# Sparse graph attention on one core: deep and own blocks take turns, first own blocks are weighed by VectorE, and several small steps come later

## The chip, the cores and the metric

The kernel runs on one core of one Trainium2 chip. A time is the device time of one execution in microseconds (us). TensorE (PE in the profile) multiplies matrices, VectorE (DVE) and ScalarE (ACT) work element by element, GpSimd (POOL) here mostly issues indirect DMAs (gathers and scatters of rows by a list of indices), and SyncE (SP) issues plain DMAs. Each engine takes its instructions in the order in which they were written, and waits in front of one whose inputs or buffers are not ready.

## The reference

`x` is 16 x 1024 x 512, `adj` is 1024 x 1024 of zeros and ones, and the same `adj` holds for all 16 batches. There are 8 heads of 64.

```
q = (x @ Wq + bq), k = (x @ Wk + bk), v = (x @ Wv + bv)      # per batch, 8 heads of 64
scores = q . k / 8 + (1 - adj) * -1e9
attn = softmax(scores)
out = attn @ v
x = layernorm(x + out @ Wo + bo)                              # no weight, eps 1e-5
```

`adj` is thin: most queries have few keys, some have dozens. So the kernel never forms the 1024 x 1024 scores.

## The kernel before, in words

**Blocks.** Queries are ranked by their number of keys and cut into 8 tiles of 128. Tile t has `OWN[t]` *own blocks*, (2, 1, 2, 3, 4, 5, 5, 7): own block i holds the i-th key of each of the 128 queries, so keys and values are gathered by one indirect DMA (`kvg`, L1230) and the query tile is read once. What queries of tiles 6 and 7 have beyond that is packed into `BLOCKS` = 1 and 5 *deep blocks* of 128 (query, key) pairs. A deep block also gathers its queries (`qg`, L1184), and its 128 rows are added into the right queries by two TensorE products with a 0/1 matrix (`add_up`, the `sum` at L1301 and L1302). Tile 1 has one key per query and needs no scores. That makes 34 blocks for batches 0, 1 and every odd batch, 32 for the other even ones (their tile 0 is handled with the next batch's), 530 in all.

**A block's way.** `products` multiplies q and k (DVE, `qk`, L1251), `scores` sums by head (DVE, L1255), `exponentials` takes exp (ACT, L1266), `weigh` multiplies the gathered values by it: either 8 ScalarE instructions, one for each head (L1276), or one VectorE instruction (L1280); `by_act` (L1268) decides. For an own block `add_own` then adds it to the tile's sum (DVE, L1292); for a deep block `add_up` does it on TensorE. After a tile's last block `normalise` divides, and `turn` transposes the result (PE, `poT`, L1336) for the product with Wo (`po`, L790), which `finish` and `complete` turn into the output: residual, `ysq` sum of squares, `variance`, `power` (a POOL instruction, L1113), `shift`, `norm_out` and a scatter (L1125).

**Fronts.** For later batches the kernel meanwhile computes q, k and v: `load_x` gathers a tile of x (POOL, L1001), `transpose_x` transposes it (`pxT`, L748), and `pair(b, j)` makes k and v of two tiles at once by a Strassen-like scheme of 7 half products into the accumulators `x`, `z` and `pp` (L947), with ScalarE and VectorE taking sums in between (`out_e`, `out_w`, `out_g`, `out_k1`, `out_v1`, `out_v0`; L960 to L979), and q by a plain product (`pq`, L790). In the pair with j = 0 the tile 1 has no q product from batch 1 on, and even batches from 2 on have no q product for tile 0 either. k and v go to DRAM, from where the blocks gather them. `mean_pe` (L858) is one product that takes the mean of a batch's v (used for queries without keys); its row goes to DRAM by SP, and only then is the batch marked in `set_up`, without which none of its blocks may be gathered.

**Order.** All order is written out by a loop over turns (L1470): `n` runs from -39 to the end, and turn n works on block n. In a turn come: exp of block n+3, products of n+4, gathers up to n+8 (up to n+11 when the fronts are done), VectorE's weighing of n+1, the own sum of n, scores of n+4, `normalise` if a tile began, then what `later(k, ...)` put k turns ahead, ScalarE's weighing of n+2, what `later_last` put there, and `add_up` of n. Last, TensorE's other work is dealt out: each turn adds its `paced` share to a `credit`, and units of fronts or of `po` are written while the credit is positive; things in `urgent` (transposes, the mean) come in between. A unit whose inputs' turn has not come (`ready`) ends the dealing for that turn. Generators (`edges`, `bias_setup`, `ranks`, `lookups`), which build the key lists in the turns before block 0, advance by one `yield` a turn.

The last pair of a batch thus sets `mean_pe` two turns after its second `send`, `load_x` is called in the turn after the transposes that free its buffer, and at the end of each batch come the 5 deep blocks of tile 7 in a row.

Of the kernel before, what the change touches and what calls it, by code (L numbers as in the profile page):

```python
# [177 lines left out]
def kernel(  # L178
# [75 lines left out]
    with ExitStack() as main:  # L254
# [139 lines left out]
        def bias_setup():  # L394
            bk_bc = work.tile([P, D], F32, tag="y", name="bk_bc", bufs=Y_BUFS)
            broadcast(bk_bc, bk)
            yield
            n4 = small.tile([P, NPAIR], F32, name="bk_norms", bufs=1)
            nc.vector.tensor_tensor(bk_bc, bk_bc, bk_bc, op=OP.mult)
            nc.vector.tensor_reduce(n4, bk_bc.rearrange("p (h d) -> p h d", d=P), axis=AX.X, op=OP.add)  # L400
            nc.vector.tensor_reduce(bk_norm, n4, axis=AX.X, op=OP.max)
            n8 = small.tile([P, HEADS], F32, name="bq_norms", bufs=1)
            nc.vector.tensor_tensor(bk_bc, bq_bc, bq_bc, op=OP.mult)
            nc.vector.tensor_reduce(n8, bk_bc.rearrange("p (h d) -> p h d", d=HD), axis=AX.X, op=OP.add)
            nc.vector.tensor_reduce(bq_norm, n8, axis=AX.X, op=OP.max)
            yield
            pb = fill_psum("pb")
            nc.tensor.transpose(pb[:, 0:2 * NPAIR], bias_rows, ident[:2 * NPAIR, :2 * NPAIR])
            nc.tensor.transpose(pb[:, 2 * NPAIR:3 * NPAIR], bv_rows, ident[:NPAIR, :NPAIR])
            yield  # L410
            nc.vector.tensor_copy(bias_qk, pb[:, 0:2 * NPAIR])
            bv_col = one.tile([P, NPAIR], F32, name="bv_col")
            nc.vector.tensor_copy(bv_col, pb[:, 2 * NPAIR:3 * NPAIR])
            bvb = work.tile([P, NPAIR, P], F32, tag="y", name="bvb", bufs=Y_BUFS)
            nc.vector.tensor_copy(bvb, bv_col[:, :, None].to_broadcast([P, NPAIR, P]))
            yield
            pb = fill_psum("pb3")
            for c in range(NPAIR):
                nc.tensor.matmul(pb, bvb[:, c, :], W["o"][:, c, :], start=(c == 0), stop=(c == NPAIR - 1))
            yield  # L420
            nc.vector.tensor_tensor(bo_bc, pb, bo_bc, op=OP.add)
# [209 lines left out]
        def edges(t):  # L631
# [38 lines left out]
                nc.vector.tensor_tensor(check[:, 2 * NT + 1:2 * NT + 2], ranked[:, t, 1:2], st[:, 0:1], op=OP.subtract)  # L670

            nc.vector.tensor_scalar(deg, ranked[:, t, 1:2], -float(K), 0.0, op0=OP.add, op1=OP.max)
            yield
            po = fill_psum(f"poff_{t}")
            nc.tensor.matmul(po[:, 0:1], before, deg, start=True, stop=True)
            yield
# [66 lines left out]
        def transpose_x(b, t):  # L743
            def pe():
                xs = X.pop((b, t))
                p = fill_psum(f"pxT_{b}_{t}")
                for c in range(NPAIR):
                    nc.tensor.transpose(p[:, ts(c, P)], xs[:, ts(c, P)], ident)  # L748

                def out():  # L750
                    XT[b, t] = work.tile([P, D], F32, tag="xT", name=f"xT_{b}_{t}", bufs=4)
                    nc.scalar.copy(XT[b, t], p)
                    n = b * NT + t + 3
                    if t == 0 and b >= PAIRED_FROM:
                        if not merged(b):
                            BOTH[b // 2] = work.tile([P, 2, NPAIR, P], F32, tag="place", name=f"both_{b}", bufs=1)
                        nc.scalar.copy(
                            BOTH[b // 2].rearrange("p w c (h n) -> p h c w n", h=2)[:, b % 2],
                            p.rearrange("p (c w n) -> p c w n", c=NPAIR, w=2),
                        )  # L760
                        sq = work.tile([P, D], F32, tag="ysq", name=f"sq_x_{b}", bufs=1)
                        nc.scalar.activation(sq[0:LONE, :], xs[0:LONE, :], AF.Square, accum_out=x_norm[0:LONE, b:b + 1])
                    if b * NT + t in STORED:
                        nc.sync.dma_start(residual[b * NT + t], xs)
                        later(2, lambda: load_x(n // NT, n % NT))
                    else:
                        load_x(n // NT, n % NT)
                    if t % 2 and (b, t) != (0, 1):
                        later(1, combine)

                def combine():
                    s = [work.tile([P, HD2], F32, tag=f"s{i}", name=f"s{i}_{b}_{t}", bufs=1 + i // 4) for i in (1, 2, 3, 4)]
                    x0, x1 = XT[b, t - 1], XT[b, t]
                    nc.vector.tensor_tensor(s[0], x1[:, 0:HD2], x1[:, HD2:D], op=OP.add)
                    nc.vector.tensor_tensor(s[2], x0[:, 0:HD2], x1[:, 0:HD2], op=OP.subtract)
                    nc.vector.tensor_tensor(s[1], s[0], x0[:, 0:HD2], op=OP.subtract)
                    nc.vector.tensor_tensor(s[3], x0[:, HD2:D], s[1], op=OP.subtract)
                    SX[b, t // 2] = s

                later(1, out)  # L780

            return [(TRANSPOSE, pe, lambda: (b, t) in X)]
# [24 lines left out]
        def pair(b, j):  # L807
# [25 lines left out]
            def send(i):  # L833
                assert b < PAIRED_FROM or gathered[0] >= start[max(0, b // 2 * 2 - 2)]
                kv = KV[b, tt[i]]
                rows, base = kv_of(b)
                for lo, hi in ((0, LONE), (LONE + P, 2 * P)) if b and tt[i] == 0 else ((tt[i] * P - (LONE if b and tt[i] == 1 else 0), None),):
                    hi = lo + P if hi is None else hi
                    part = slice(0 if lo % P == 0 or hi - lo == P else LONE, P if hi - lo == P or lo else LONE)
                    later(1, lambda lo=lo, hi=hi, part=part: nc.sync.dma_start(rows[base + lo:base + hi, :], kv[part, :]))  # L840
                R["sent"] = R.get("sent", 0) + 1
                if R["sent"] == 2:
                    later(1, add_v)
                    if j == NT // 2 - 1:
                        later(2, lambda: urgent.append(mean_pe))

            def add_v():
                kv = [KV.pop((b, t))[:, D:] for t in tt]
# [136 lines left out]
            units = []  # L985
            units += unit("x", lambda: a(0, 0), B11, True, out_e, None)
            units += unit("p6", s(2), T2, True, out_w, None)
            units += q0
            units += unit("x", lambda: a(0, 1), B21, False, lambda: out_k(0, R["x"]), "e")
            units += unit("p7", s(3), T3, True, out_g, None)  # L990
# [94 lines left out]
        def complete(b, t, p, plain):  # L1085
# [46 lines left out]
            if single:  # L1132
                late = 1 if fronts else 0
                later(2 + late, variance)
                later(3 + late, power)
                later(4 + 2 * late, shift)
                later_last(5 + 2 * late, norm_out)
            elif second:
                later(3, variance)
                mate_shift, mate_norm_out = half.pop()[1]  # L1140

                def powers():
                    nc.gpsimd.tensor_tensor(
                        st2[:, :, 3:4], st2[:, :, 2:3], neg_half[:, :, None].to_broadcast([P, 2, 1]), op=OP.pow
                    )

                def shifts():
                    mate_shift()
                    shift()

                later(4, powers)
                later(6, shifts)
                later_last(6, mate_norm_out)
                later_last(7, norm_out)
            else:
                later(3, variance)
                mine = half[0]
                mine.append((shift, norm_out))

                def alone():  # L1160
                    if half and half[0] is mine:
                        half.pop()
                        power()
                        later(2, shift)
                        later_last(3, norm_out)

                later(6, alone)
# [2 lines left out]


        KG, QG, PV, PSUM, QT, RDEN, V1 = {}, {}, {}, {}, {}, {}, {}
        blocks = [(b, t, i) for b in range(B) for t in tiles_of(b) if t != ONE_KEY for i in range(OWN[t] + BLOCKS[t])]
        start = [min(n for n, block in enumerate(blocks) if block[0] == b) for b in range(B)] + [len(blocks)]

        def load_more():
# [90 lines left out]

        def by_act(n):  # L1268
            b, t, i = blocks[n]
            return 0 < i < OWN[t] or n < total - NBT and (n % 2 == 0 or n < NBT // 2)  # L1270

        def weigh(n):
            v, pv = KG.pop(n), PV[n]
# [174 lines left out]
        with tc.manual_schedule():  # L1448
# [21 lines left out]
            while n < total or plan or rest or urgent or done or finishing or spilled or lone_tiles or not guarded:  # L1470
# [50 lines left out]
                    reload(*spilled.pop(0), reloads)  # L1521
                    reloads, last_reload = reloads + 1, n
                first_unit = True
                while credit > 0 or urgent:
                    if urgent and not (first_unit and fronts):
                        urgent.pop(0)()
                        continue
                    if (
# [2 lines left out]
                    ):  # L1531
                        finishing = finish(*done.pop(0))
                        last_finish = n
                    units = finishing or fronts
                    if not units:
                        if urgent:
                            urgent.pop(0)()
# [52 lines left out]
```

## Time and profile before

| | us |
|---|---|
| median of 3 runs (1903.19 to 1907.76) | 1906.49 |
| the profiled execution's own time | 1892.33 |
| its span, first to last instruction | 1890.4 |
| PE busy | 1815.1 (96%) |
| DVE busy | 1700.6 (90%) |
| ACT busy | 1531.7 (81%) |
| POOL busy | 1267.4 (67%) |
| mean granted TensorE clock | 0.989 |

Busy time is the union of an engine's instructions. A matrix product in 32-bit floats appears as two records of some 596 ns each that overlap; in the chain of waits eight records take 3.43 us, so one 128x512x128 product occupies TensorE for about 0.86 us. "Idle before, and what ended it" is the time in which an engine had nothing running, put down to the instruction whose end let it go on.

### The profile page before, as it was taken

The page shows a single profiled execution, that of the slowest core. Times are in us where ns is not written, and L with a number is a line of the kernel's source. Part 1 is how long each engine was busy: PE and PEld are TensorE (multiplying, and loading weights), DVE is VectorE, ACT ScalarE, POOL GpSimd, SP SyncE. Part 2 cuts the span into 40 slices and gives each one's busy share as a digit, 9 for nine tenths or more (in the row PEclk, how much of TensorE's full clock was granted, in tenths as well). Part 3 has the DMA queues.
Part 4 walks back from the last instruction along what each step waited for, and adds up shares of the span by engine and source line. Part 5 has one row for each costly group of instructions (what it writes and reads, how often), then busy time and mean ns, then how long its engine had stood idle before and what let it go on. Part 6 is the DMA issues. An engine that isn't in the chain of part 4 may idle for free. (4 is left out here: it accounts for less than half of the span.)

```text
span 1890.4 us, 25101 instructions
## 1 busy us (share of the span) xinstructions
PE 1815.1 (96%) x5149; PEld 878.2 (46%) x5149; DVE 1700.6 (90%) x3484; ACT 1531.7 (81%) x6016; POOL 1267.4 (67%) x1189
## 2 busy tenths in 40 slices
PE   7989999999999999999999999999999999999995
PEld 3434444444545454444445444444445444444442
DVE  6888889999999999899899989899999999997874
ACT  3627869979888988979798978989898989886794
POOL 1367766777677676757677676767666777656774
PEclk9989999999999999999999999999999999999997
DMA  7357787988889898888889898999889899989993
GB/s 280 114 168 226 233 307 227 315 295 294 308 287 316 305 328 283 305 288 307 312 292 335 271 334 274 314 304 310 301 307 326 293 356 310 314 277 340 334 319 117
DMA packets 188149, 544.63 MB, mean 288 GB/s; under 512 B 32602, under 2 KB 32622, under 8 KB 187986
## 3 DMA queue, kind: packets, MB, share of 16 engines
q0 software_dynamic: 116400, 382.82, 60.6%
q1 hardware_dynamic: 68510, 154.30, 21.8%
q10 hardware_dynamic: 3076, 5.82, 0.9%
q14 instruction: 120, 0.98, 0.2%
q8 instruction: 43, 0.70, 0.1%
HBM read 419.52 MB, written 144.34 MB: 298 GB/s over the span
## 5 line engine op out<-in xcount | busy, mean ns | idle before, releaser
L1276 ACT ACTIVATE pv<-kvg,pv 128x64 f32<-128x64 f32 x3432 | 864.6, 340 | 0.0
L1230 POOL DMA_INDIRECT kvg<-kv_pair,place_row x462 | 526.7, 1140 | 258.0 <-ACT pv L1276 73.3
L790 PE MATMUL po<-wo,oT 128*128 128x512 f32 x816 | 380.1, 596 | 1.0 <-ACT oT L1340 0.9
L790 PE MATMUL pq<-wq,xT 128*128 128x512 f32 x792 | 368.9, 597 | 0.4 <-DVE g L966 0.4
L1255 DVE TENSOR_REDUCE s<-qk 128x8 f32<-128x512 f32 x530 | 360.2, 680 | 7.5
L1251 DVE TENSOR_TENSOR qk<-qt,kvg 128x512 f32<-128x512 f32 x434 | 296.4, 683 | 22.2 <-DMA kvg<-kv_pair,place_row 22.1
L947 PE MATMUL pp<-t,s 128*128 128x512 f32 x504 | 237.4, 593 | 2.7 <-ACT sq_k L800 1.7
L947 PE MATMUL x<-b,xT 128*128 128x512 f32 x504 | 237.8, 594 | 0.8 <-ACT e L960 0.8
L790 PEld LDWEIGHTS po<-wo,oT 128*128 128x128 f32 x816 | 152.6, 191 | 166.8 <-issue 153.9
L1292 DVE TENSOR_TENSOR pv<-pv,pv 128x520 f32<-128x520 f32 x329 | 228.0, 693 | 0.7 <-ACT pv L1276 0.6
L790 PEld LDWEIGHTS pq<-wq,xT 128*128 128x128 f32 x792 | 149.2, 192 | 166.4 <-issue 155.0
L1266 ACT ACTIVATE pv<-s,absent 128x8 f32<-128x8 f32 x434 | 126.3, 293 | 79.8 <-DVE s L1255 76.2
L1001 POOL DMA_INDIRECT x<-in_x_dram,asked_row x120 | 130.2, 1085 | 88.3 <-PE pxT L748 40.5
L1125 POOL DMA_INDIRECT out_dram<-y,asked_row x129 | 144.8, 1122 | 35.7 <-issue 19.8
L800 ACT ACTIVATE sq_k<-kv 128x128 bf16<-128x128 f32 x512 | 150.9, 301 | 6.0 <-DVE kv L970 6.0
L947 PEld LDWEIGHTS pp<-t,s 128*128 128x128 f32 x504 | 94.2, 190 | 114.1 <-issue 101.4
L947 PEld LDWEIGHTS x<-b,xT 128*128 128x128 f32 x504 | 94.3, 191 | 111.5 <-issue 106.5
L1184 POOL DMA_INDIRECT qg<-q_rows,query_row x96 | 106.9, 1114 | 36.5 <-issue 24.7
L947 PE MATMUL z<-b,s 128*128 128x512 f32 x252 | 119.1, 595 | 6.5 <-DVE kv L975 6.5
L1029 POOL DMA_INDIRECT y<-in_x_dram,asked_row x93 | 104.5, 1124 | 27.5 <-issue 25.8
L947 PE MATMUL z<-t,s 128*128 128x512 f32 x252 | 120.0, 599 | 0.0
L947 PE MATMUL pp<-t,xT 128*128 128x512 f32 x252 | 118.4, 592 | 0.0
(276 smaller groups left out, 2766.7 us busy)
## 6 DMA issues: line engine op xcount, KB each, us to landing
kv_pair<-kv SPq DMA_DIRECT2D x98, 512.0 KB
q_rows<-q SPq DMA_DIRECT2D x106, 256.0 KB
qt<-q_rows SPq DMA_DIRECT2D x98, 256.0 KB
residual<-x SPq DMA_DIRECT2D x36, 256.0 KB
y<-residual SPq DMA_DIRECT2D x36, 256.0 KB
kv_rows<-kv SPq DMA_DIRECT2D x15, 512.0 KB
kvg<-kv_pair,place_row POOLq DMA_INDIRECT x462, 6.5
kv_pair<-kv SPq DMA_DIRECT2D x28, 256.0 KB
```

Source lines behind the costliest of these rows:

```text
L790: nc.tensor.matmul(p, lhs(c), w[:, c, :], start=(c == 0), stop=(c == NPAIR - 1))
L800: nc.scalar.activation(sq, s[:, ts(h, P)], AF.Square, scale=scale, accum_out=sums[:, h:h + 1])
L947: nc.tensor.matmul(R[bank], l[:, ts(c, P)], right[:, c, :], start=(first and c == 0), stop=(c == 1), skip_group_check=True,)
L1001: nc.gpsimd.indirect_dma_start(out=y, out_offset=None, in_=x_rows, in_offset=bass.IndirectOffsetOnAxis(ap=asked_row[:, t:t + 1], axis=0), ...
L1125: nc.gpsimd.indirect_dma_start(out=out_rows[b, t], out_offset=bass.IndirectOffsetOnAxis(ap=rows, axis=0), in_=y, in_offset=None, element_o ...
L1184: nc.gpsimd.indirect_dma_start(out=q, out_offset=None, in_=q_rows[b % ROWS], in_offset=bass.IndirectOffsetOnAxis(ap=rows, axis=0))
L1230: nc.gpsimd.indirect_dma_start(out=KG[n], out_offset=None, in_=rows, in_offset=bass.IndirectOffsetOnAxis(ap=(place_row if b else key_row)[ ...
L1251: nc.vector.tensor_tensor(QK[n], q, KG[n][:, 0:D], op=OP.mult)
L1255: nc.vector.tensor_reduce(S[n], QK.pop(n).rearrange("p (h d) -> p h d", d=HD), axis=AX.X, op=OP.add)
L1266: nc.scalar.activation(PV[n][:, D:], S.pop(n), AF.Exp, bias=bias)
L1276: nc.scalar.activation(pv[:, ts(h, HD)], v[:, ds(D + h * HD, HD)], AF.Copy, scale=pv[:, D + h:D + h + 1])
L1292: nc.vector.tensor_tensor(PV[b, t], PV[b, t], pv, op=OP.add)
```

## The change

1. `blocks_of`: from batch 1 on, own and deep blocks of one tile alternate. Tile 6 becomes o o o d o o, tile 7 o o d o d o d o d o d o; the last block of a batch is an own block.
2. `by_act`: the first own block of a tile is always weighed by VectorE. Before, ScalarE had it when its number was even (70 of the 105). Own blocks after the first stay with ScalarE. Deep blocks go to ScalarE when the batch's number plus i is even (two of six in even batches, four in odd ones), none in the last batch: 44 in place of 30. Together 373 blocks are weighed by ScalarE and 157 by VectorE, after 429 and 101.
3. `mean_pe` comes 4 turns after the second `send` in place of 2.
4. The product for the lists of keys (`poff`) and the bias product (`pb`, L419) each come two turns later in their generators.
5. The gather of x that follows a transpose comes one turn later.
6. While fronts run, `power`, `shift` and `norm_out` of an output tile each come one turn later.
7. In a pair with j = 0 the first of the two x transposes takes the place of tile 0's q product, and that q product and the second transpose come where tile 1's would stand, between the two products into `z`.
8. In the last three turns before the end of the blocks no unit of `po` is dealt, so the last sums are written ahead of it.

```diff
@@ bias_setup
-            yield
+            for _ in range(3):
+                yield
             pb = fill_psum("pb3")
@@ edges
-            yield
+            for _ in range(3):
+                yield
             po = fill_psum(f"poff_{t}")
@@ transpose_x
-                        load_x(n // NT, n % NT)
+                        later(1, lambda: load_x(n // NT, n % NT))
@@ pair, send
-                        later(2, lambda: urgent.append(mean_pe))
+                        later(4, lambda: urgent.append(mean_pe))
@@ pair
             units += unit("p6", s(2), T2, True, out_w, None)
+            if j == 0:
+                q0, q1, xt = xt[:1], q0 + xt[1:], []
             units += q0
@@ complete
                 late = 1 if fronts else 0
                 later(2 + late, variance)
-                later(3 + late, power)
-                later(4 + 2 * late, shift)
-                later_last(5 + 2 * late, norm_out)
+                later(3 + 2 * late, power)
+                later(4 + 3 * late, shift)
+                later_last(5 + 3 * late, norm_out)
@@ blocks
-        blocks = [(b, t, i) for b in range(B) for t in tiles_of(b) if t != ONE_KEY for i in range(OWN[t] + BLOCKS[t])]
+        def blocks_of(b, t):
+            own, deep = list(range(OWN[t])), list(range(OWN[t], OWN[t] + BLOCKS[t]))
+            if b == 0 or not deep:
+                return own + deep
+            spread = max(1, len(own) // (len(deep) + 1))
+            left = len(own) - spread * len(deep)
+            for j, i in enumerate(deep):
+                own.insert(left + j * (spread + 1), i)
+            return own
+        blocks = [(b, t, i) for b in range(B) for t in tiles_of(b) if t != ONE_KEY for i in blocks_of(b, t)]
@@ by_act
             b, t, i = blocks[n]
-            return 0 < i < OWN[t] or n < total - NBT and (n % 2 == 0 or n < NBT // 2)
+            if i < OWN[t]:
+                return i > 0
+            return n < NBT // 2 or (n % 2 == 0 if b == 0 else b < B - 1 and (b + i) % 2 == 0)
@@ the loop
-                while credit > 0 or urgent:
+                last_sums = total - 3 <= n < total
+                while credit > 0 and not last_sums or urgent:
@@
-                    units = finishing or fronts
+                    units = [] if last_sums else finishing or fronts
```

## The prediction, on record before the changed kernel ran

> **What bounds the kernel now.** I read the page first, then TensorE's waits, then VectorE's and POOL's, then single stretches in order of time.
>
> ```profile
> PE 1815.1 (96%) x5149; PEld 878.2 (46%) x5149; DVE 1700.6 (90%) x3484; ACT 1531.7 (81%) x6016; POOL 1267.4 (67%) x1189
> ...
> PE   7989999999999999999999999999999999999995
> ```
>
> TensorE is busy 1815 of 1890 us and the change leaves its products as they are. So the most that can be won is its idle time, 75 us, plus what a halved clock costs; the digits put the idle time at both ends, some in between.
>
> ```profile
> PE sum L1301 <- DVE pv L1280: 13.8, 6, 3.7
> ...
> PE z L947 <- DVE kv L975: 6.5, 6, 2.4
> PE pm L858 <- DVE vsum L854: 5.6, 4, 1.9
> PE pb L419 <- DVE bvb L415: 5.6, 1, 5.6
> ...
> PE poff L675 <- DVE est L672: 2.1, 1, 2.1
> ```
>
> These are TensorE's own waits (total us, times, longest): 33.6 us, and 1.3 more before `pm` by another line, stand before the deep sums, the second `z`, the mean, the bias product and the key list's product. Nearly all are waits for VectorE. Next, what VectorE and POOL wait for.
>
> ```profile
> POOL kvg L1230 <- ACT pv L1276: 88.0, 72, 6.2
> ...
> POOL x L1001 <- PE pxT L748: 40.5, 19, 13.6
> ...
> DVE qk L1251 <- DMA kvg<-kv_pair,place_row: 25.6, 13, 4.9
> ```
>
> The order of time joins them. At the end of batch 5:
>
> ```profile
> 804.94 0.69 DVE L1251 TENSOR_TENSOR qk<-qt,kvg 128x512 f32<-128x512 f32 x1 [4.28 <-DMA kvg<-kv_pair,place_row]
> ...
> 805.55 0.69 DVE L1280 TENSOR_TENSOR pv<-kvg,pv 128x512 f32<-128x512 f32 x1
> ...
> 806.29 1.22 PE L1301 MATMUL sum<-pv,sums 128*128 128x256 f32 x2 [3.75 <-DVE pv L1280]
> ```
>
> VectorE stands 4.28 us before the next batch's first block because its gather is late; the weighing of a deep block is queued behind; TensorE waits 3.75 us for it. The same picture is at 907, 1118 and 1628 us (1.89, 2.82, 2.51). Last, busy time by stretch (PE, PEld, DVE, ACT, POOL, granted clock, DMA share, GB/s):
>
> ```profile
> 130.00:140.00 10.00, 5.06 (x6) 2.19 (x7) 9.17 (x15) 1.51 (x6) 7.87 (x8) 0.68 0.78 252
> 300.00:350.00 50.00, 48.76 (x140) 22.57 (x139) 49.12 (x99) 46.76 (x195) 33.19 (x33) 1.00 0.83 282
> 850.00:900.00 50.00, 49.93 (x139) 23.31 (x138) 49.16 (x98) 47.71 (x195) 38.11 (x35) 1.00 0.88 309
> 1250.00:1300.00 50.00, 48.11 (x136) 22.61 (x135) 49.36 (x101) 44.06 (x173) 36.85 (x35) 1.00 0.90 297
> 1550.00:1600.00 50.00, 46.81 (x132) 21.92 (x131) 49.52 (x93) 46.52 (x189) 32.32 (x30) 0.97 0.93 321
> ```
>
> VectorE is close behind: where it fills 49 us of 50, TensorE idles.
>
> **The change, part by part** (against the profiled execution, 1892.33 us, 14.2 below the median of the runs).
>
> *Key list and bias product, two turns later.* Before: waits of 2.1 and 5.6 us, each followed by a lower clock (0.68 in the first stretch above). The 8 records of `pb` took 6.41 us against 3.43 elsewhere (3.0 lost), those after `poff` 1.6 more than elsewhere. Together 12.3. In the new order of TensorE's instructions three products of 1.72 us stand ahead of `pb` that stood behind, 5.2 against the wait of 5.6. But right after `pb` a transpose needs a PSUM bank that VectorE frees only with `q`, some three blocks' scores later (1.36 us each), and VectorE is 92% busy there. I take half, **-6** (-12 to -2).
>
> *Alternation.* The four boundary waits sum to 11.0 us; the granted clock is 0.97 over the 50 us around two of them (802 and 1629), some 1.7 us lost each, 3.4 in all: 14.4 at most. Five deep blocks in a row ask POOL for ten gathers in five turns (1.14 us each by the page, 11.4 of some 16 us), with the next batch's first ones behind; now every second block needs two. A deep sum no longer stands last in its batch, so a late first gather hits an own block's addition. What stays: gathers wait for buffers that ScalarE frees (88.0 us above), and that isn't changed. **-10** (-14.4 to 0).
>
> *The mean, two turns later.* Its waits on TensorE are 6.9 us. But the batch may be gathered only after it. Counted in the order written by either kernel, the first gather moves from 8 turns ahead of the batch to 6 in batch 13, from 7 to 5 in 14, from 7 to 6 in 15, from 8 to 7 in batch 0; in the others the mean is early enough. Block 0's product comes 4 turns ahead, so in batch 14 one turn (3.2 us; 32 blocks take 102.2 us) is left for a gather that lands 6.5 us after issue: VectorE waits at least 3.3 us there, about 1 each in 13 and 15. SP's queue has q, k and v stores and `qt` loads behind the mean's row; SP is mostly waiting anyway. **-5.5** (-6.9 to 0) for the mean and **+3** (0 to 8) for the gathers.
>
> *First pair's products.* The six `z` waits: in odd batches (2.36 and 1.18) q's four products, 3.4 us, now lie between the two `z` products and cover them; in even ones (0.58, 0.98, 1.03) there is no q product, and only a transpose of 0.44 us comes in, so half stays. **-4** (-5 to 0). In odd batches the copy `e` loses that cover between the two `x` products; even batches had none before and show one wait of 0.8 us: **+1** (0 to 2).
>
> *Weighing.* ScalarE loses 56 blocks of 8 x 0.252 us, 113 us, VectorE gains 56 x 0.683 = 38 us, in 1750 us of blocks. VectorE's 139 us of waits are the cover: some 80 are for TensorE and vanish where it comes later. If that cover is gone, all 38 land on the path; in the other direction ScalarE's copies come sooner, worth 3 at most by its waits in TensorE's list. Nearest rows: from 200 to 1700 us VectorE is busy 46.8 of 50 and TensorE idles 1.0; in the four stretches above it is busy 49.3 and TensorE idles 1.6. The added 33 us in these 30 stretches are 1.1 each, 0.44 of the way, of 0.6 x 30 = 17 us: **+7** (-3 to 38).
>
> *Tail.* Before, a `po` product lies between the last sums (5.8 us, partly at half clock), after waits of 1.9 and 0.9. Now it is written ahead. But the last block is an own one: 8 x 0.25 on ScalarE and an addition of 0.69 in place of one VectorE weighing and a sum, 1.1 more. **-3** (-6 to +2).
>
> *x gathers and powers, a place later.* POOL no longer stands for transposes (40.5 us, most of it off the path; x is used about eight turns on): **-1** (-4 to 0). Powers: outputs hold their buffers one turn longer; at most five are asked for at once: 0 (0 to 2), covered by POOL's 33% idle.
>
> Sum: -6 -10 -5.5 +3 -4 +1 +7 -3 -1 = **-18.5**: 1873.8 for such a profiled execution, **1888** on the median (1906.49 - 18.6).
>
> **Two rules of the skill.** The clock fell after waits of 2.1 and 2.5 us and not after the 2.8 at 1118. The Trainium skill (TensorE: Matmul & The Clock Gate, part 1) gives an idle window of about 3.4 us that runs freely; by it only the waits of 5.6 and 3.75 would cost clock, and the clock's part of the sum above would be 4.7 in place of 8.0. Against the change speaks GPSIMD Engine Reference (8. Key points): GpSimd contends with VectorE instructions that have two SBUF inputs. The weighing is one; no row here separates it, and POOL's gathers have a median of 1.02 us in the middle of such instructions. By an estimate from that page, one gather stretched per added weighing would be POOL time only, hidden at 67%.
>
> **The rivals.**
> *VectorE becomes the bound.* Speaking for it: 49 us of 50 in the stretches shown. Against: TensorE's gaps are few and mostly at batch ends. If all 38 us reach the path, -18.5 -7 + 38 = +12.5: about 1919. It decides from the point where over 25.5 of the 38 us are not covered.
> *The waits only move.* TensorE waits elsewhere on a VectorE that is as late as before (most of its waits name VectorE). Then lead-in, mean, `z` and half of the sums give nothing, -6 -5.5 -4 -5 = 20.5 less: +2, about 1908.
> *All waits go and VectorE's extra work is covered.* Upper ends -12 -14.4 -6.9 -5 -6 -4, with +3 and +1: -44, about 1862.
> That the change doesn't do what it says I exclude but for batch 0, which keeps its order: in the new order of instructions the sums are apart and VectorE has 56 more.
>
> **How the numbers follow.** Forecast 0.47 (its own range 1876 to 1898), all waits go 0.20, waits only move 0.16, VectorE the bound 0.17. Three tenths of a per cent, 5.7 us, is about what a measurement can tell from no change. Faster: the forecast, the strong case and a little of the third, 0.69; same 0.14; slower 0.17. For eight in ten the range goes from 1864, inside the strong case, to 1919, the slow rival's value.
>
> **What would show it.** Right: TensorE's wait at the sums under 4 us in all, at `pm` and `pb` under 2; VectorE's waits for `kvg` at batch ends gone but for batches 13 to 15; VectorE busy about 1738, ScalarE about 1420. The deep sums wait as before: alternation step wrong. New TensorE waits on VectorE at `pxT` after 130 us: lead-in half too high. More stretches with VectorE over 49 of 50 and TensorE under 48: the slow rival. It would also be wrong if batches 13 to 15 lose more than 8 us.

## The result, and the profile after

The changed kernel took 1929.42 us (median of 6 runs, 1925.86 to 1937.23), the kernel before beside it 1906.17 us (6 runs, 1902.95 to 1910.45). The ratio is 1.0128, 95% interval [1.0104, 1.0153]: some 24 us slower, where 18 us faster was forecast, and 10 us beyond the range.

One thing is needed to read the rest. The runs were made in groups, each on one chip with the kernel before beside it, and the kernel before did not take the same time in all of them: 1890.9 and 1890.6 us in two groups, 1909.4, 1907.5 and 1906.2 in three, 1925.7 in the last. Its profile (1892.33) is of the first level, the profile after (1927.37) of the second. So 35 us between these two profiles is partly the chip. Ratios are taken within a group only, and where two traces are set against each other in time, the changed kernel is stood in for by *u_lead* (below): it differs in the lead-in (the key list's and the bias product) alone, has the changed kernel's ratio (1.0134) and was profiled at the first level.

The page of after, busy time and TensorE's busy tenths:

```profile
PE 1828.6 (95%) x5149; PEld 882.3 (46%) x5149; DVE 1735.9 (90%) x3540; ACT 1432.8 (74%) x5568; POOL 1273.3 (66%) x1189
...
PE   8988999999999999999999999999999989999896
```

VectorE and ScalarE are where they were forecast (1738 and 1420). TensorE is not: in 1925.6 us it idles 97, where it idled 75, and the same 5149 records take 13.5 us more. *u_lead* shows the same on the faster level: 88.0 us idle against 75.3, and 1826.1 busy against 1815.1, at a granted clock of 0.982 against 0.989. So of its 23.7 us, 12.7 are new gaps and 11.0 are products that took longer at a lower clock.

TensorE's own waits after (total us, times, longest):

```profile
PE z L949 <- DVE kv L977: 14.9, 6, 6.4
PE pxT L750 <- DVE q L823: 7.2, 4, 3.7
...
PE po L792 <- DMA oTs<-spill: 6.8, 1, 6.8
...
PE pp L949 <- ACT oT L1358: 4.0, 1, 4.0
PE pp L949 <- DVE q L823: 4.0, 1, 4.0
...
PE sum L1319 <- DVE pv L1298: 1.0, 2, 0.7
```

The waits that the change was forecast to take are gone: those of the deep sums for VectorE fell from 13.8 to 1.0 us, and `pm`, `pb` and `poff` are no longer in the list. So the signs that the prediction had named for being right came true, and the kernel is slower all the same. In the place of these waits stand others: `z` went from 6.5 to 14.9 us (6.4 of it in one wait at 151 us) instead of halving, and `pxT` and `pp` now wait for `q`. Summed over the list, waits that name VectorE are 47.4 us before and 43.6 in *u_lead*: they moved. Those that name ScalarE rose from 4.7 to 13.2 us, and those that name a DMA from 9.1 to 16.2. Most of the latter rise is one wait, that before `po` for a tile kept in DRAM and loaded again (`oTs` from `spill`), in the last batch (0.9 before, 7.1 in *u_lead*). *u_weigh* below has it too (5.7 us) and is faster than the kernel before beside it, so it does not decide by itself; what makes that load late was not tried.

POOL's waits after:

```profile
POOL kvg L1246 <- DVE pv L1298: 101.9, 45, 6.3
...
POOL x L1005 <- DMA residual<-x: 26.3, 8, 9.3
...
POOL more L1221 <- DMA kv_pair<-mean: 9.4, 1, 9.4
POOL kvg L1246 <- DMA kv_rows<-mean: 6.7, 1, 6.7
```

Gathers that stood for a buffer held by VectorE's weighing did so 16 times for 36.2 us before, now 45 times for 101.9; those that stood for ScalarE's went from 88.0 us to 61.9. And POOL now stands in front of the gathers of batches 0 and 15 until the mean's row is in DRAM. In batch 0 this costs little: the first gather starts at 118.17 us, after 117.81 before, where it had stood 10.3 us for another load (`others`).

Where does TensorE lose? One place in order of time, around 1317 us, VectorE first and then TensorE:

```profile
1317.24 0.68 DVE L968 TENSOR_TENSOR g<-pp,w 128x512 f32<-128x512 f32 x1
1317.84 0.68 DVE L1267 TENSOR_TENSOR qk<-qt,kvg 128x512 f32<-128x512 f32 x1
1318.43 0.71 DVE L1298 TENSOR_TENSOR pv<-kvg,pv 128x512 f32<-128x512 f32 x1
1319.07 0.69 DVE L1310 TENSOR_TENSOR pv<-pv,pv 128x520 f32<-128x520 f32 x1
1319.68 0.67 DVE L1271 TENSOR_REDUCE s<-qk 128x8 f32<-128x512 f32 x1
...
1320.34 0.68 DVE L977 TENSOR_TENSOR kv<-z,g 128x512 f32<-128x512 f32 x1
```

```profile
1315.31 1.88 PE L949 MATMUL pp<-t,xT 128*128 128x512 f32 x4
1321.07 1.22 PE L949 MATMUL z<-b,s 128*128 128x512 f32 x1 [3.89 <-DVE kv L977]
```

No VectorE instruction in these rows waited. Four instructions of blocks, one of them a weighing (of a deep block), stand between `g` and the `kv` that TensorE needs, and TensorE stands for 3.89 us. The busy time there, and around the first gather of batch 14 (PE, PEld, DVE, ACT, POOL, granted clock, DMA share, GB/s):

```profile
1300.00:1310.00 10.00, 10.00 (x33) 5.06 (x31) 9.90 (x20) 7.37 (x30) 7.97 (x9) 1.00 0.85 273
1310.00:1320.00 10.00, 7.19 (x20) 2.58 (x18) 9.90 (x21) 8.41 (x30) 7.97 (x9) 0.98 0.96 354
1320.00:1330.00 10.00, 8.93 (x20) 4.84 (x21) 7.57 (x17) 5.21 (x25) 7.48 (x8) 0.68 0.95 331
```

```profile
1650.00:1660.00 10.00, 5.96 (x23) 3.36 (x22) 5.35 (x12) 5.90 (x23) 7.39 (x8) 0.87 0.91 306
1660.00:1670.00 10.00, 10.00 (x21) 4.93 (x21) 9.12 (x20) 7.16 (x41) 6.05 (x7) 0.78 1.01 387
```

VectorE fills 9.90 of 10 us in two stretches running, TensorE falls behind it, and then runs at 0.68 of the clock: the gap is paid a second time. Over 50 us the same place looks harmless:

```profile
300.00:350.00 50.00, 47.88 (x131) 21.80 (x130) 49.30 (x101) 41.84 (x173) 34.25 (x33) 1.00 0.81 274
...
1300.00:1350.00 50.00, 46.11 (x134) 23.42 (x132) 45.39 (x88) 38.80 (x155) 36.74 (x35) 0.93 0.93 313
...
1650.00:1700.00 50.00, 45.96 (x128) 22.52 (x127) 43.12 (x88) 36.35 (x151) 31.38 (x29) 0.93 0.86 294
```

VectorE's share from 1300 to 1350 is 45.39, below its average from 200 to 1700 us (47.1), since it is busy only 7.57 and 8.13 of 10 us after the gap. Between 200 and 1700 us the stretches of 50 us with VectorE at 49 or more went from 4 to 10, but of these only 2 (before: 1) have TensorE under 48. So the prediction's sign for the slow rival hardly shows it.

Stretches of 10 us do. Between 200 and 1700 us TensorE idles 30.6 us before and 36.7 in *u_lead*. In the stretches where VectorE is busy 9.5 or more of 10 this rose from 20.3 to 25.6 us, in all others from 10.3 to 11.2. The stretches with a granted clock under 0.95 went from 3 to 8. In *u_weigh*, and in the changed kernel with 66 us of VectorE's work taken away (*nv_after*), the idle time in the full stretches is 13.6 and 15.9 us, and 1 and 2 stretches have the lower clock. The other half of the new gaps lies outside 200 to 1700 us, where the wait for the reloaded tile is.

The second place is the start of batch 14:

```profile
1651.88 0.15 DVE L1120 SCALAR_TENSOR_TENSOR stats<-stats 128x1 f32<-128x1 f32 x1
1656.64 0.70 DVE L1267 TENSOR_TENSOR qk<-qt,kvg 128x512 f32<-128x512 f32 x1 [4.61 <-DMA kvg<-kv_pair,place_row]
...
1658.04 0.68 DVE L823 SCALAR_TENSOR_TENSOR q<-pq,bq_bc 128x512 f32<-128x512 f32 x1
```

VectorE stands 4.61 us for a late gather, `q` is queued behind, and TensorE then waits 4.04 us for `q`. (That the gather causes the wait does not hold up: see *u_mean*.) Taking the time from each batch's first scores to the next one's in *u_lead* and in before, batches 13, 14 and 15 are longer by 2.9, 6.0 and 7.8 us, batches 1 to 12 by 10 in all, and the end after the last block is 4.1 shorter. So most of the loss lies in the last three batches.

### The profile page after: what moved, and what is told of

Read it like the earlier page. It is cut to its first block, busy times and chain, and to the rows that moved or that the text cites. A ratio compares the mean times of both kernels' runs of the same rounds, so it can differ in the third digit from the quotient of the medians.

```text
span 1925.6 us, 24618 instructions
## 1 busy us (share of the span) xinstructions
PE 1828.6 (95%) x5149; PEld 882.3 (46%) x5149; DVE 1735.9 (90%) x3540; ACT 1432.8 (74%) x5568; POOL 1273.3 (66%) x1189
## 5 line engine op out<-in xcount | busy, mean ns | idle before, releaser
L1294 ACT ACTIVATE pv<-kvg,pv 128x64 f32<-128x64 f32 x2984 | 751.5, 338 | 3.7 <-ACT pv L1282 1.9
L1246 POOL DMA_INDIRECT kvg<-kv_pair,place_row x462 | 526.3, 1139 | 303.4 <-DVE pv L1298 84.3
L1005 POOL DMA_INDIRECT x<-in_x_dram,asked_row x120 | 135.7, 1131 | 82.1 <-issue 26.3
L1129 POOL DMA_INDIRECT out_dram<-y,asked_row x129 | 149.1, 1156 | 36.1 <-issue 23.3
L802 ACT ACTIVATE sq_k<-kv 128x128 bf16<-128x128 f32 x512 | 150.8, 299 | 14.9 <-DVE kv L972 11.2
L949 PE MATMUL z<-b,s 128*128 128x512 f32 x252 | 123.0, 611 | 15.0 <-DVE kv L977 14.9
```

The source lines that it names most:

```text
L802: nc.scalar.activation(sq, s[:, ts(h, P)], AF.Square, scale=scale, accum_out=sums[:, h:h + 1])
L949: nc.tensor.matmul(R[bank], l[:, ts(c, P)], right[:, c, :], start=(first and c == 0), stop=(c == 1), skip_group_check=True,)
L1005: nc.gpsimd.indirect_dma_start(out=y, out_offset=None, in_=x_rows, in_offset=bass.IndirectOffsetOnAxis(ap=asked_row[:, t:t + 1], axis=0), ...
L1129: nc.gpsimd.indirect_dma_start(out=out_rows[b, t], out_offset=bass.IndirectOffsetOnAxis(ap=rows, axis=0), in_=y, in_offset=None, element_o ...
L1246: nc.gpsimd.indirect_dma_start(out=KG[n], out_offset=None, in_=rows, in_offset=bass.IndirectOffsetOnAxis(ap=(place_row if b else key_row)[ ...
L1294: nc.scalar.activation(pv[:, ts(h, HD)], v[:, ds(D + h * HD, HD)], AF.Copy, scale=pv[:, D + h:D + h + 1])
```

## The experiments

The theory after the result: **VectorE's added weighings reach the path**, as it was already the engine that most of TensorE's waits name. Rivals: the mean's delay makes gathers late; alternation only moves waits; the lead-in got worse. All kernels with "undone" are the changed kernel with that part as before; all with "alone" are the kernel before with that part only. The changed kernel itself was not run again in these groups: on the first chip *u_lead* stands for it.

### One part undone at a time (kernel before: 1890.87 us)

*u_lead*, list and bias products as before:

```diff
-            for _ in range(3):
-                yield
+            yield
             pb = fill_psum("pb3")      # and the same ahead of po = fill_psum(f"poff_{t}")
```

> The changed kernel, with the key list's and the bias product where they were. The prediction gave their move 6 us: 1933 to 1937. If the waits only moved, as the changed kernel's TensorE waits of 5.0 us at 121 us and 6.4 at 151 say, within 3 us of 1929.

1.0134 [1.0102, 1.0167]: no difference from the changed kernel (1.0128) is seen. The two were on different chips, and the difference is 1 us, uncertain by some 8, so the ratios alone do not rule out the 6 us forecast. The waits speak against them. In *u_lead* the waits are 3.2 us at `poff` and 1.6 at `pb`; with the delay both are gone, and TensorE waits 4.97 us before `pp` at 121 and 6.38 before `z` at 151 instead.

*u_mean*, the mean two turns after the second `send` again:

```diff
-                        later(4, lambda: urgent.append(mean_pe))
+                        later(2, lambda: urgent.append(mean_pe))
```

> The changed kernel, with the mean of v again two turns after its batch's last send. Theory M (the later mean holds back the gathers of batches 0, 13, 14 and 15, which lost 8.8, 3.2, 7.2 and 7.0 us, 26 of the 35 us between the two profiled executions): about 1905 to 1915, 15 to 25 us faster than the changed kernel's 1929, with POOL's waits of 9.4, 6.7 and 9.3 us before its gathers gone. Theory W (VectorE's 56 further weighings are the cost): 1922 to 1930, and TensorE waits for the mean's product again, some 7 us.

1.0067 [1.0049, 1.0085]. TensorE's waits at the mean are back, and yet the kernel is about 0.7% faster than *u_lead* beside it:

```profile
PE pm L860 <- DVE vsum L856: 6.0, 4, 2.9
```

```profile
DVE qk L1267 <- DMA kvg<-kv_pair,place_row: 8.5, 12, 1.6
```

VectorE's longest wait for a gather falls from 4.9 us to 1.6, and POOL no longer stands for the mean's row. In the changed kernel the delay costs more than it gives. But its price is not where the late gathers are: batches 13 and 14 are as long as in *u_lead* (3.0 and 6.1 us more than before), and only batch 15 gives back much, 6.2 of some 12 us. At the start of batch 14 no gather is late now, and TensorE still waits 3.08 us for `q`:

```profile
1641.26 3.62 PE L949 MATMUL pp<-t,xT 128*128 128x512 f32 x4 [3.08 <-DVE q L823]
```

*u_order*, no alternation (`if b >= 0 or not deep:` in `blocks_of`):

> The changed kernel, with own blocks first and deep blocks last in every tile again, the new rule for who weighs kept. If the alternation is worth the 10 us that the prediction gave it, this is about 10 us slower than the changed kernel, 1935 to 1945, and TensorE waits for VectorE's weighing at the sums again, some 14 us. If the alternation itself costs (gathers and weighings that no longer come in runs), 1910 to 1925.

1.0059 [1.0035, 1.0083]: also about 0.7% faster than *u_lead*, though the waits at the sums are back in full:

```profile
PE sum L1319 <- DVE pv L1298: 16.6, 9, 5.6
```

So 15 us of waits that the change took away here came back elsewhere in it, with interest. Of the some 12 us by which this kernel beats *u_lead*, 7.4 again lie in batch 15: what *u_mean* and *u_order* win is in part the same.

*u_weigh*, the rule of weighing as before:

```diff
-            if i < OWN[t]:
-                return i > 0
-            return n < NBT // 2 or (n % 2 == 0 if b == 0 else b < B - 1 and (b + i) % 2 == 0)
+            return 0 < i < OWN[t] or n < total - NBT and (n % 2 == 0 or n < NBT // 2)
```

> The changed kernel, with the old rule for who weighs (first own blocks and deep blocks by the parity of their number), the alternation kept. Theory W: VectorE's busy time falls by some 35 us to about 1700, and the time by 15 to 30 us to 1900 to 1914. Theory M: 1920 to 1930, since batches 1 to 12 lost only 16 us together and VectorE's weighing is only a part of that.

0.9966 [0.995, 0.9982]: the whole loss is gone. VectorE's busy time fell further than the 35 us expected, to 1680.0: with alternation the deep blocks of tile 7 all get even numbers, and the old rule gives them all to ScalarE. That leaves VectorE 59 weighings, not 101, so more is undone here than the change had done. It shows in the batches: 1 to 12 are 13.4 us shorter than in the kernel before, while 14 and 15 are still 5.8 and 7.1 longer. The `z` waits, untouched by the edit, fall from 14.9 (9.8 in *u_lead*) to 4.3 us:

```profile
PE z L949 <- DVE kv L977: 4.3, 4, 1.8
```

### Which weighings, and how much of it is the mean (kernel before: 1909.36 us)

*only_weigh* is the new rule alone (157 weighings by VectorE); *w_deep* the changed kernel with the old rule for deep blocks (129); *w_own* with the old rule for first own blocks (87); *wm* has rule and mean both as before (59).

```diff
             if i < OWN[t]:
-                return i > 0
+                return i > 0 or n < total - NBT and (n % 2 == 0 or n < NBT // 2)    # w_own
```

> The kernel before, with nothing but the new rule for who weighs: VectorE has 157 blocks after 101, 38 us more work, all else as before. If the number counts as in the changed kernel (1.6% for 98): 1.009. If all of the 38 us reach the path: 1.020. If VectorE's waits cover it as the prediction had it: 1.004.

1.011 [1.0072, 1.0147]: the rule alone costs 21 us on this chip (14 to 28 by the interval) of the 38 us that it adds to VectorE. This is the clean measure of the step: nothing else differs.

> The changed kernel with only the deep blocks' old rule (72 with ScalarE), all first own blocks with VectorE: VectorE weighs 129. If only the number counts: 1.008. If the first own blocks' place counts: 1.010 to 1.013. If the deep ones count: about 0.998.

1.0098 [1.0067, 1.0129].

> The changed kernel with only the first own blocks' old rule (70 of 105 with ScalarE), deep blocks by the new one: VectorE weighs 87 blocks. The changed kernel has 157 and the kernel with the old rule in the new order 59 (in that order all deep blocks of tile 7 have even numbers and go to ScalarE, so it is fewer than the 101 of before). If only the number counts (1.6% for 98 weighings): 1.001. If the place counts (a first own block falls on a change of tile, where VectorE also divides): 0.996 to 0.999. If the deep ones count: 1.010 and more.

1.0024 [0.9999, 1.005]. With two thirds of the first own blocks (70 of 105) back at ScalarE little loss is left; with 28 deep blocks back nearly 1% is. But these two kernels differ in the number of weighings too (87 and 129).

> The changed kernel with both undone: the old rule for who weighs and the mean two turns after the last send. Undone alone they gave 0.9966 and 1.0067 of the kernel before, after 1.0128 for the changed kernel. If the two costs add up: 0.990 to 0.992. If the later mean hurts only where VectorE is late, 0.995 to 0.998.

1.0038 [1.0013, 1.0063], above both values expected (0.990 to 0.998), which rested on *u_weigh*'s 0.9966 from another chip.

### Parts alone (kernel before: 1907.47 us)

*u_weigh_b* and *wm_b* are *u_weigh* and *wm* again, *only_mean* and *only_order* the mean's delay and the alternation alone.

> The changed kernel with the old rule for who weighs, once more, beside its neighbours on one chip. It gave 0.9966 of the kernel before on a chip where that takes 1891 us. If the place of the chip has no part in it: 0.995 to 0.999. If the gain is that chip's: 1.000 to 1.006.

1.0033 [1.0013, 1.0054], against 0.9966 at the faster level: the intervals don't meet. That with the old rule the rest of the change gains 0.3% on one chip and loses 0.3% on another is measured, not explained.

> The same with the mean two turns after the last send. The first measure, on a chip where the kernel before takes 1909 us, was 1.0038. If the later mean is good where VectorE is not late: 0.3 to 0.8% above the run beside it. If the mean does not matter there: equal to it within 0.3%. If it costs as in the changed kernel: 0.4 to 0.7% below it.

1.005 [1.0026, 1.0075]. Beside *u_weigh_b* no difference by the mean's delay is seen once VectorE has 59 weighings (0.2%, uncertain by 0.3); with 157 it cost 0.7%.

> The kernel before with nothing but the later mean. The prediction's terms are -5.5 for the mean's waits and +3 for the gathers: 0.9987. If the late gathers of batches 0, 13, 14 and 15 count as in the changed kernel (0.6%): 1.003 to 1.006.

1.0025 [1.0001, 1.0049]: alone it costs about 5 us (0 to 9). It was to give 2.5 net.

> The kernel before with nothing but the alternation; its own rule for who weighs then gives all five deep blocks of tile 7 in batches 1 to 14 to ScalarE, so VectorE weighs 59 blocks after 101, 29 us less. If the alternation is worth the 10 us of the prediction, and VectorE's lesser work as much as its greater work cost (1.1% for 56): 0.985 to 0.990. If only VectorE's work counts: 0.992. If the alternation itself costs and VectorE's work gains: 0.997 to 1.003.

1.0025 [0.9998, 1.0053]: no gain, although it also takes some 20 us of busy time from VectorE (1679.9, 59 weighings). For the same reason it is not the alternation by itself that is measured. Its waits, in a profiled run of 1924.22 us, longer than the median of 1910.62:

```profile
PE z L947 <- DVE kv L975: 14.9, 7, 5.2
```

```profile
DVE pv L1303 <- ACT pv L1287: 15.9, 20, 1.6
```

The sums' waits are nearly gone (4.4 us for ScalarE, 0.5 for VectorE), those at `z` are 14.9 us, and VectorE's additions now wait for ScalarE's weighing 20 times (0.6 us in all before).

### The amount of VectorE work (kernel before: 1890.58 us)

*nv_after* and *nv_before* are the changed kernel and the kernel before without the 96 additions that sum v over a batch (0.69 us each, 66 us of VectorE); they leave out part of v's mean, which only queries without keys use:

```diff
                 else:
-                    for v in kv:
-                        nc.vector.tensor_tensor(VSUM[b], VSUM[b], v, op=OP.add)
+                    pass
```

> The changed kernel without the additions of v after the first pair of a batch (96 VectorE instructions of 0.688 us, 66 us; the mean of v is then that of two tiles only, which is left out on purpose and only queries without keys would show). If VectorE is the bound of the changed kernel, the place where its extra work lands: 20 to 45 us faster than the changed kernel's 1.0128, 0.990 to 1.002 of the kernel before. If VectorE's extra work only cost through its place at the tile changes: within 8 us of the changed kernel, 1.008 to 1.013.

0.9987 [0.9971, 1.0003]. Against *u_lead* (1.0134, on another chip of the same level) that is some 28 us back for 66 taken away. Batches 14 and 15 are still 5.0 and 7.6 us longer than in the kernel before.

> The kernel before without the same additions (the same part of the mean left out). If VectorE has room there, as the equal times of 59 and 87 weighings say: 0.996 to 1.000. If VectorE bounds the kernel before as well, in proportion to the changed one (1.1% for 38 us): 0.980 to 0.986.

0.9939 [0.9922, 0.9956]: 11.5 us back for the same 66. Not all of it is VectorE's time: these additions feed the mean's product, and TensorE's waits before `pm` fall from 6.9 us to 0.2 without them, while the changed kernel had none there to lose. So a VectorE microsecond was worth at most 0.17 us in the kernel before, and 0.42 in the changed one.

*place_mid* is the kernel before with 56 more VectorE weighings, as many as the new rule adds, at the middle own block of tiles 4 to 7:

```diff
+            if 0 < b < B - 1 and t > 3 and i == OWN[t] // 2:
+                return False
             return 0 < i < OWN[t] or n < total - NBT and (n % 2 == 0 or n < NBT // 2)
```

> The kernel before with 56 more VectorE weighings, as many as the changed kernel has, but elsewhere: the middle own block of tiles 4 to 7 in batches 1 to 14. If the amount of VectorE's work counts: 1.008 to 1.014, as with the new rule alone (1.011). If it counts that a first own block falls on a change of tile, where VectorE also divides: 1.000 to 1.005.

1.0068 [1.005, 1.0086]: 13 us for 38, or 0.34 us for each.

*others* is the changed kernel with rule, alternation and mean all as before, so with only the list and bias products, x gathers, powers, first pair and tail changed:

> The changed kernel with three parts undone: who weighs, the alternation and the mean. What is left is the list and bias products, the x gathers, the powers, the first pair's products and the last sums. The prediction gave them -6, -1, 0, -3 and -3 us: 0.993. If their waits only move: 0.997 to 1.002. If one of them costs: above 1.003.

0.9974 [0.9962, 0.9986]: 4.9 us faster than the kernel before. Only this version of the change and *u_weigh* (0.9966 on one chip, 1.0033 on another) came out under it; this one was run on one chip only. Batches 14 and 15 are as before (0.5 us longer, 0.8 shorter). Here the waits at `z` do fall:

```profile
PE sum L1317 <- DVE pv L1296: 12.6, 6, 7.2
...
PE pm L860 <- DVE vsum L856: 6.8, 6, 2.8
...
PE z L949 <- DVE kv L977: 2.7, 3, 1.1
```

### Amount or place, on one chip (kernel before: 1925.65 us)

*only_weigh* and *place_mid* had been on different chips. Both again, side by side:

> The kernel before with the new rule of weighing alone (157 VectorE weighings in place of 101, 38 us more of VectorE), beside the next kernel on one chip. Theory 'the amount counts': the same ratio as the next kernel within 0.3%, 1.006 to 1.011. Rival 'the place counts too' (the first own blocks stand at a tile's change, where a sum has just begun and POOL waits for the buffer): at least 0.4% above the next kernel, 1.011 or more.

1.0098 [1.0067, 1.0129], 18.9 us.

> The kernel before with the same number of added VectorE weighings (56, 157 in all), at the middle own blocks of tiles 4 to 7, the same kernel as the one that took 1.0068 on another chip. 'The amount counts': within 0.3% of the kernel with the new rule. 'The place counts too': 1.005 to 1.008, 0.4% or more under it.

1.0043 [1.0018, 1.0067], 8.3 us. Both have 157 weighings and the same VectorE busy time (1729.6 and 1731.6). At the middle blocks each added microsecond costs 0.22 us here (0.34 on the other chip); at the first own blocks 0.50. The intervals touch at 1.0067, so about half of the rule's cost lies in where the weighings stand, and this much is likely rather than certain. POOL's waits, the first line of *only_weigh_b* (profiled at 1945.69 us), the second of *place_mid_b* (at 1947.01, the longest of its runs):

```profile
POOL kvg L1230 <- DVE pv L1282: 107.8, 42, 5.7
```

```profile
POOL kvg L1230 <- DVE pv L1282: 70.0, 34, 4.6
```

Gathers stand longer for VectorE's weighing when it is that of a tile's first block. That this is what costs was not tried by itself.

## Why the prediction was wrong

Each step beside what the runs gave for it:

| step | forecast, us | measured | |
|---|---|---|---|
| list and bias | -6 | 0, uncertain by 8 (*u_lead* against the changed kernel) | other waits in the place of these, 4.97 at `pp` and 6.38 at `z` |
| alternation | -10 | +5 alone (-0 to +10), with 42 fewer VectorE weighings | sums' waits 13.8 to 1.0 as forecast; `z` and `q` waits in their place |
| mean | -5.5 and +3 | +5 alone (0 to 9) | `pm` waits gone as forecast; batch 15 longer by 6.2 (*u_lead* against *u_mean*) |
| first pair | -4 and +1 | in *others* `z` 6.5 to 2.7 | in the changed kernel 14.9 |
| weighing | +7 | +19 to +21 alone | above |
| tail | -3 | -4.1 after the last block (*u_lead*) | the size fits, the cause does not show: 3.9 and 4.5 shorter in *only_order* and *place_mid*, which lack the step, 4.7 longer in *others*, which has it |
| all of list, bias, first pair, tail, x, powers | -14 + 1 | -4.9 (*others*) | four tenths of it |

Starting from the forecast of -18.5, the weighing adds 13, the alternation 15, the mean 7.5, list and bias 6, the remaining parts 2: +25, near the measured 24. That the sum fits is partly luck: the parts come from several chips, and they are not independent. With 157 weighings, undoing the mean or the alternation gives 0.7% each, much of it the same 6 to 7 us in batch 15; with 59, undoing the mean gives nothing that is seen (*wm_b* beside *u_weigh_b*). That a delay reaches TensorE when VectorE has no time to make it good would explain this; it was not shown by itself.

**The step that failed first is "Weighing +7".** Alone, on two chips, the rule made the kernel before slower by 21 and 19 us, and it is the one edit whose undoing takes the whole loss away (0.9966), or most of it (1.0033, 0.0095 less than the changed kernel's ratio, on another chip). The mechanism was named, as the slow rival; the term was mis-sized: 19 to 21 us, inside the step's own bounds (-3 to 38) and nearly three times its value. The alternation was off by as much or more (15 us), but its measure also holds a change in the number of weighings. Two things went wrong in the working of the weighing:
- It took a straight line through TensorE's idle time in stretches of 50 us. That average hides what happens: VectorE is full for 20 us, TensorE stands 3.9 us, then VectorE idles. The two places shown lie in stretches where VectorE shows 43 to 46 of 50.
- It counted idle time only. In *u_lead* 11.0 of 23.7 us are products at a lower clock, as gaps came where there had been none.

The cover that it named, VectorE's 139 us of waits, is real but partial: of each microsecond of VectorE work, 0.17 or less (*nv_before*) to 0.34 (*place_mid*) reached the path in the kernel before, 0.42 in the changed one, 0.5 or more where the rule puts it. By the rival's own condition (over 25.5 of the 38 us not covered) this was not enough to make the kernel slower. It did, since the gains that it had to eat up were not there.

**The mean (-5.5 and +3).** The sentence "it would also be wrong if batches 13 to 15 lose more than 8 us" came true: 16.7 us in *u_lead*, which also hold other costs. With the mean undone the same batches still lose 10.7 (3.0, 6.1 and 1.6), so the delay's share there is 6, nearly all of it in batch 15. The counted turns were right (in batch 14 VectorE waited 4.61 us, at least 3.3 forecast), but that wait was not the price: without it TensorE waits 3.08 us at the same product instead of 4.04. The step left out POOL, which in batch 15 stands 9.4 us in front of its gathers until the mean's row has landed; in *u_mean* this wait is gone, and TensorE's wait for the reloaded tile is 3.6 us in place of 7.1. How the one leads to the other was not shown. What lengthens batch 14 stays open too: each single part undone leaves it 5.8 us or more longer (*u_mean*, *u_order*, *u_weigh*), and with all three undone it is as before (*others*).

**Alternation (-10).** What was to be gained was the wait's place, not its cause. TensorE waited at the sums because VectorE was late; after the change it waits at `z`, `pxT` and `pp`, mostly for the same engine (47.4 us of waits name it before, 43.6 in *u_lead*). That is the rival "the waits only move", which was given 0.16 and applied to half of the sums only; by these lists it held for them all, and for the lead-in.

**The two rules weighed in the prediction.** The wait of 2.44 us at 957 and that of 3.89 at 1317 were each followed by a lower clock (0.83 and 0.68 in the next stretch of 10 us). For the first:

```profile
960.00:970.00 10.00, 9.32 (x20) 4.01 (x19) 6.22 (x14) 8.37 (x35) 8.05 (x7) 0.83 0.87 275
```

The Trainium skill (TensorE: Matmul & The Clock Gate, part 1) asks for about one idle window of 3.4 us. The wait of 3.89 is longer than that; that of 2.44 is not, and here, as before, it was enough. On GpSimd's contention with VectorE instructions of two SBUF inputs, the Trainium skill (GPSIMD Engine Reference, 8. Key points) gives no size. With 56 more of these the mean of the 462 gathers from `kv_pair` is 1139 ns in the changed kernel, 1146 in *only_weigh* and 1150 in *place_mid*, after 1140: 1% at most.

## What to carry to other kernels

Where most of TensorE's waits name one other engine, as here, do not count a wait that an edit moves as won, and expect work added to that engine to cost, even if it has long waits of its own; price such work by taking a known amount away (here 66 us of additions gave 11.5 us back, and 28 once the engine was fuller). Read cover in stretches as short as the queue in front of the waiting product, 10 us here: over 50 us the engine that has just caused a gap can look idle. And count a gap on TensorE with the lower clock that may follow it: here 12.7 us of new gaps came with 11.0 us of slower products.

## What the runs showed of the hardware

The kernel before, unchanged, took 1890.6 to 1925.7 us in the medians of the groups, 1.9% apart, more than the whole effect studied here; a part's ratio can change its sign between them (*u_weigh* 0.9966 and 1.0033). The granted clock goes along: its median over the runs of the kernel before is 0.990 in the group of 1890.6 us and 0.986 in that of 1925.7.
